# Copying the sources' columns of one tile in every 12th group on VectorE and on ScalarE, in a graph layer's edge loop

## The chip, the core and the metric

The kernel runs on one core of a Trainium2 chip. The metric is the device time of one execution in microseconds (us). In the profiles PE is TensorE's matmul array and PEld its weight loads, DVE is VectorE, ACT is ScalarE, POOL is GpSimd and SP is SyncE. L372 is line 372 of the kernel.

## The reference

A graph network's layer over 12500 nodes with 64 features and 212500 edges with 32 features, in float32. The edges come sorted by their destination `dst`.

```python
msg_in = concatenate([x[src], x[dst], edge_attr_32], axis=-1)        # 212500 x 160
messages = relu(msg_in @ mW1 + mb1) @ mW2 + mb2
aggregated = segment_sum(messages, dst, num_segments=12500)
u = relu(concatenate([x, aggregated], axis=-1) @ uW1 + ub1) @ uW2 + ub2
out = layernorm(x + u, axis=-1, eps=1e-05)
```

`src` is random over the nodes, so the rows `x[src]` have to be gathered, edge by edge.

## The kernel before

**Tiling.** Edges are cut into tiles of 128 (P) and tiles into groups of three (TG), so that there are 554 groups (G). All sorted destinations of a group lie in a window of 32 (W) nodes. A group's work has these steps:

- *gather* (L142 to L153): POOL issues one indirect DMA for each tile, L145, which brings the 128 source rows of 64 numbers to `own.s`, one edge on each partition. `own.s` is a ring of 20 groups (RING). The gather of group g waits for the copy of group g - 20 out of the ring (`copy_by[g - RING]`). The loop issues it 16 groups ahead (AHEAD).
- *onehot* (L321, work at L324): DVE writes, beside each gathered row, 32 numbers that say which node of the window the edge goes to.
- *turn* (L354): PE transposes the three tiles of `own.s`, 96 columns each (64 features and 32 of the one-hot), into PSUM, L360; ACT copies the result to `own.st` and takes the row sums of the one-hot part, L372.
- *hidden* (L381): PE multiplies the turned group with the weights, L392, and ACT applies relu, L401.
- *sums* (L411): PE multiplies hidden values with the one-hots, L419 and L422; DVE adds the result to `agg` and the window's counts to a row of `xc`, L431 and L432.
- *windows* and *places* (L306 and L291), once for four groups: PE computes the destinations' part for four windows, L310, DVE copies it into the weights `own.wm`, L315; DVE reads the places of the next four windows and copies their nodes' columns, L303.

**Copied tiles.** The features of all nodes also lie transposed in SBUF, in `xc`, one column a node. In some groups, the keys of COPIED, the third tile (ONE) isn't gathered. Its 128 columns are copied one at a time from `xc` to a tile `own_f`, by DVE with `tensor_copy` (L349) or by ACT with `activation` (L350). The source's number comes from a register: a load (L343) fills eight registers (REGS) from `cols_sb`. Each way has a range of groups, BY_DVE and BY_ACT, whose step is also the number of groups over which the 128 columns are spread, and two tiles `own_f`. The copying ends three groups (SLACK) before the group itself:

```python
at = k - (g - SLACK - way.step)
if not 0 <= at < way.step:
    continue
f, used, ahead = source_columns(g), g - 2 * way.step, held[engine]
for r in range(at * P // way.step, (at + 1) * P // way.step):
    if r % REGS == 0:
        ...
    column = f[:D, r : r + 1], xc[:D, bass.ds(ahead[r % REGS], 1)]
```

For a copied group the gather loop leaves out that tile (L150). ACT's copy of the turned group becomes two instructions, one for the 64 feature rows of two tiles and one for the 32 one-hot rows of three (L369). In *hidden* PE makes two products for the copied tile, one of `own_f` with the weights and one of the 64 remaining rows of `own.st` (L389).

**Order.** The order of each engine's work is written out by hand. In iteration k of the main loop come, in this order: the load of edge features (SP), *places* when k leaves 1 over 4, *onehot* of group k + 1, a PE step, the gathers of group k + 16, and the columns that are due in k (`copies_of`, L334). The PE step (`step`, L502) holds *turn* of group k, *hidden* of k - 2 and *sums* of k - 4 in one stretch with one wait ahead and one semaphore at its end; *windows* is added to it for every fourth k. When it is done, ACT does the copy of turn and the relu of hidden, and DVE the addition of sums, and the copies to `own.wm` if there are any. So DVE's queue reads: addition of step k, columns of k, *places* if due, one-hot of k + 2, addition of step k + 1. PE's step k + 2 waits for that one-hot. ACT's queue reads: copy, relu, columns. Every 22 groups or so, when all edges of 512 nodes are done, an *update* (L438) computes the output of those nodes, in steps between the others.

Of the kernel before, what the change touches and what calls it, by code (L numbers as in the profile page):

```python
# [31 lines left out]
G = (E + GE - 1) // GE  # L32
# [11 lines left out]
NEAR_GROUPS = 24  # L44
SHORT = 10
ONE = TG - 1
BY_DVE = range(44, G - 16, 16)
BY_ACT = range(48, G - 16, 24)
COPIED = {**dict.fromkeys(BY_DVE, (ET.DVE, BY_DVE)), **dict.fromkeys(BY_ACT, (ET.Activation, BY_ACT))}
SLACK = 3  # L50
REGS = 8
# [30 lines left out]
class Own:  # L82
# [4 lines left out]
    def __init__(self, nc, ctx):  # L87
        def on(name, *shape, of=nc.sbuf_tensor):
            return ctx.enter_context(of(name, list(shape), F32)).ap()
# [6 lines left out]
        self.f = {way: [on(f"own_f{len(way)}_{i}", P, P) for i in range(2)]  # L96
                  for way in (BY_DVE, BY_ACT)}
        self.ident = on("own_ident", P, P)
# [797 lines left out]
```

## Time and profile before

| | |
|---|---|
| median of 3 runs | 2696.31 us (2695.68 to 2698.4) |
| the profiled execution | 2690.72 us, span 2688.9 us |
| mean granted clock of TensorE | 0.787 |
| gathers L145 | 1609, mean 944 ns |
| copied columns | 3968 on DVE (mean 143 ns), 2688 on ACT (mean 193 ns) |
| register loads L343 | 496 on DVE (median 608 ns), 336 on ACT (median 551 ns) |
| turned tiles L360 | 1661 |

A row of the groups reads: line, engine, operation, what it writes and reads, how often, then busy us and mean ns of one, then the idle time of the engine just ahead of it and who ended most of it. A row of the timeline reads: start and duration in us, engine, line, operation, how many were merged into the row, and in brackets the idle time ahead of it and its end. The ends of matmuls are modelled. DVE and ACT overlap their short instructions, so that eight columns take less than eight times the mean of one.

The page's slices show how even the run is:

```profile
PE   1356666666666675766666656666566666677667
PEclk9777787778777777777777878787777777787779
```

The first line is PE's busy share in 40 equal slices in tenths, the second the granted clock, in tenths of full speed. From the third slice to the last two, nothing changes.

### The profile page before, as it was taken

How to read it: one execution, taken by the hardware profiler on the slowest of the kernel's cores; microseconds unless marked ns; L12 is line 12 of the kernel's file. 1: busy time of each engine (PE TensorE's matmuls, PEld its weight loads, DVE VectorE, ACT ScalarE, POOL GpSimd, SP SyncE). 2: the span in 40 equal slices, each digit the busy share in tenths (PEclk: the TensorE clock that was granted, in tenths of full speed). 3: DMA queues.
4: the chain of work that ended last, by engine and by line, in shares of the span. 5: the costliest groups of instructions: out<-in, count | busy, mean ns of one | idle time of the engine just before them, and what ended most of it. 6: DMA issues, size and time to landing. Idle time of an engine off the chain costs nothing.

```text
span 2688.9 us, 45023 instructions
## 1 busy us (share of the span) xinstructions
PE 1687.1 (63%) x9545; PEld 1457.1 (54%) x9545; DVE 1060.2 (39%) x7163; ACT 827.3 (31%) x4455; POOL 1519.4 (57%) x1616
## 2 busy tenths in 40 slices
PE   1356666666666675766666656666566666677667
PEld 0355555555555565655555555555555555565555
DVE  4124344344443444443434434434344343443423
ACT  0123333333333333333333333333333333333322
POOL 7565555555555555555555555555555555565550
PEclk9777787778777777777777878787777777787779
DMA  3211111111111111111111111111111111111110
GB/s 80 58 44 32 35 32 36 31 36 32 35 37 32 34 34 35 31 36 32 37 31 35 34 32 34 34 34 34 35 32 34 33 37 31 35 35 35 33 34 14
DMA packets 71878, 95.29 MB, mean 35 GB/s; under 512 B 32633, under 2 KB 40076, under 8 KB 71596
## 3 DMA queue, kind: packets, MB, share of 16 engines
q0 software_dynamic: 51488, 52.80, 10.3%
q1 hardware_dynamic: 19193, 39.06, 5.3%
q8 instruction: 81, 1.33, 0.2%
q14 instruction: 202, 1.65, 0.2%
q10 hardware_dynamic: 914, 0.46, 0.1%
HBM read 88.90 MB, written 3.20 MB: 34 GB/s over the span
## 4 chain that ended last, share of the span: by engine, by line
PE 50%; issue 18%; another core or an unknown queue 16%; ACT 10%; ACTq 3%; DVE 3%; DMA 0%; DVEq 0%; SPq 0%
PE own_ps L422 19%; PE own_ps L392 16%; PE own_ps L360 9%; ACT own_h L401 3%; ACT own_f L350 3%; ACT own_st L372 3%; ACTq L343 2%; PE own_ps L419 2%; PE u_ps L462 2%; PE u_ps L449 1%; PE own_ps L310 1%; ACTq L350 1%; PE u_ps L450 1%; DVE agg L431 1%
## 5 line engine op out<-in xcount | busy, mean ns | idle before, releaser
L145 POOL DMA_INDIRECT own_s<-in_x,src_sb x1609 | 1518.6, 944 | 1091.0 <-ACT own_st L372 677.1
L360 PE MATMUL own_ps<-own_ident,own_s 128*96 128x128 f32 x1661 | 364.2, 341 | 906.5 <-issue 677.0
L372 ACT ACTIVATE own_st<-own_ps 96x384 f32<-96x384 f32 (+2 forms) x606 | 286.1, 472 | 1697.7 <-PE own_ps L422 1006.0
L360 PEld LDWEIGHTS own_ps<-own_ident,own_s 128*96 128x96 f32 x1661 | 224.4, 159 | 983.9 <-issue 735.6
L422 PE MATMUL own_ps<-own_s,own_h 128*128 128x128 f32 x3322 | 647.5, 343 | 0.4 <-issue 0.3
L392 PE MATMUL own_ps<-own_wm,own_st 128*128 128x128 f32 (+1 forms) x3322 | 630.8, 338 | 1.4 <-DVE own_wm L315 1.4
L392 PEld LDWEIGHTS own_ps<-own_wm,own_st 128*128 128x128 f32 (+1 forms) x3322 | 571.9, 251 | 16.5 <-issue 11.7
L431 DVE TENSOR_TENSOR agg<-own_ps,agg 128x32 f32 x554 | 105.2, 190 | 1202.7 <-ACT own_h L401 1089.6
L422 PEld LDWEIGHTS own_ps<-own_s,own_h 128*128 128x128 f32 x3322 | 525.6, 236 | 27.3 <-issue 0.3
L349 DVE COPY own_f<-xc 64x1 f32 x3968 | 428.8, 143 | 217.7 <-issue 213.2
L350 ACT ACTIVATE own_f<-xc 64x1 f32 x2688 | 304.6, 193 | 9.1 <-issue 6.2
L401 ACT ACTIVATE own_h<-own_ps 128x384 f32<-128x384 f32 x553 | 263.3, 476 | 18.4 <-PE own_ps L392 13.1
L315 DVE COPY own_wm<-own_ps 32x128 f32<-32x128 f32 x550 | 156.9, 285 | 6.8 <-issue 1.3
L324 DVE TENSOR_TENSOR own_s<-iota,dlc 128x96 f32<-128x96 f32 x554 | 135.7, 245 | 21.6 <-issue 16.7
L432 DVE TENSOR_TENSOR xc<-own_ps,xc 1x32 f32 x554 | 101.2, 183 | 27.8 <-PE u_ps L450 7.4
L419 PE MATMUL own_ps<-own_ident,own_counts 32*1 32x32 f32 x554 | 107.1, 193 | 4.2 <-ACT own_st L372 1.9
L372 ACT ACTIVATION_READ_ACCUMULATOR own_st<-own_ps 96x1 f32 (+1 forms) x554 | 106.4, 192 | 0.6
L303 DVE COPY xw<-xc 66x32 f32 x554 | 78.6, 210 | 49.2 <-issue 48.3
L419 PEld LDWEIGHTS own_ps<-own_ident,own_counts 32*1 32x1 f32 x554 | 41.3, 74 | 93.8 <-issue 47.8
L310 PE MATMUL own_ps<-w1b,xw 66*128 66x128 f32 (+1 forms) x276 | 56.9, 290 | 0.0
L462 PE MATMUL u_ps<-u,u 128*128 128x64 f32 (+1 forms) x196 | 49.1, 398 | 10.0 <-ACT u L452 10.0
L462 PEld LDWEIGHTS u_ps<-u,u 128*128 128x128 f32 (+1 forms) x196 | 47.5, 326 | 11.5 <-ACT u L452 11.3
(63 smaller groups left out, 338.5 us busy)
## 6 DMA issues: line engine op xcount, KB each, us to landing
own_st<-in_efT SPq DMA_DIRECT2D x138, 192.0 KB
own_s<-in_x,src_sb POOLq DMA_INDIRECT x1609
xin<-in_x SPq DMA_DIRECT2D x24, 128.0 KB
out<-o SPq DMA_DIRECT2D x24, 128.0 KB
xc<-in_xT SPq DMA_DIRECT2D x12, 179.2 KB
dlc_i<-in_dst_cols SPq DMA_DIRECT2D x1, 831.0 KB
xc<-in_xT SPq DMA_DIRECT2D x4, 179.5 KB
src_sb<-in_src SPq DMA_DIRECT2D x13, 50.5 KB
```

The lines of the kernel that those rows point to most:

```text
L145: nc.gpsimd.indirect_dma_start(out=s[:p, j, :D], out_offset=None, in_=x[:, :], in_offset=bass.IndirectOffsetOnAxis(ap=src_sb[:p, g * TG + ...
L315: c = nc.vector.tensor_copy(wm[g % NW][D : D + W, :], wp[i * W : (i + 1) * W, :])
L324: places_by[g] = nc.vector.tensor_tensor(own.s[g % RING][:, :, D:], iota.unsqueeze(1).to_broadcast([P, TG, W]), dlc[:, g * TG : (g + 1) * ...
L349: c = (nc.vector.tensor_copy(*column) if engine == ET.DVE else nc.scalar.activation(*column, AF.Copy))
L350: else nc.scalar.activation(*column, AF.Copy))
L360: nc.tensor.transpose(xt[:, j * P : j * P + p], s[:p, j, :], ident[:p, :p])
L372: nc.scalar.activation(t[to, c : c + m], xt[to, :m], AF.Copy, **({"accum_out": counts[to, g : g + 1]} if to.stop > D else {})), step)
L392: did.append(nc.tensor.matmul(pre[:p, j, :], edges, weights, start=i == 0, stop=i == len(parts) - 1))
L401: relu_by[g] = [nc.scalar.activation(h, pre, AF.Relu)]
L419: did = [nc.tensor.transpose(line, counts[lo:, g : g + 1], ident[lo : D + W, lo : D + W])]
L422: did.append(nc.tensor.matmul(sg, h[:p, j, :], s[:p, j, D:].unsqueeze(1).to_broadcast([p, TIMES, W]), start=j == 0, stop=j == len(sizes) - 1))
L462: nc.tensor.matmul(o_ps[:p, k], u[:, k:q:n], u2, start=True, stop=True)
```

## The change

```diff
-BY_DVE = range(44, G - 16, 16)
-BY_ACT = range(48, G - 16, 24)
+BY_DVE = range(44, G - 16, 12)
+BY_ACT = range(50, G - 16, 12)
```

G - 16 is 538. Before, DVE copies the third tile of groups 44, 60, ... 524, 31 tiles, and ACT that of 48, 72, ... 528, 21 tiles. After, DVE copies that of 44, 56, ... 536, 42 tiles, and ACT that of 50, 62, ... 530, 41 tiles. The 128 columns of a tile are spread over 12 groups in place of 16 on DVE and 24 on ACT: 10 or 11 columns a group in place of 8 on DVE and 5 or 6 on ACT. The buffers, the ring, the lead of the gathers and the size of a register load stay. `cols_sb` has a row for each copied tile and grows with their number.

## The prediction

> **What bounds it now.** I read the page's busy line, then its groups, then the table of waits, then the timeline of one stretch, row by row.
>
> ```profile
> PE 1687.1 (63%) x9545; PEld 1457.1 (54%) x9545; DVE 1060.2 (39%) x7163; ACT 827.3 (31%) x4455; POOL 1519.4 (57%) x1616
> L145 POOL DMA_INDIRECT own_s<-in_x,src_sb x1609 | 1518.6, 944 | 1091.0 <-ACT own_st L372 677.1
> L349 DVE COPY own_f<-xc 64x1 f32 x3968 | 428.8, 143 | 217.7 <-issue 213.2
> L350 ACT ACTIVATE own_f<-xc 64x1 f32 x2688 | 304.6, 193 | 9.1 <-issue 6.2
> ```
>
> No engine is full. The table of waits shows a ring of waits: POOL waits for ACT's copy of a turned group, ACT for a PE step, DVE for ACT's relu.
>
> ```profile
> DVE agg L431 <- ACT own_h L401: 1089.6, 280, 47.6
> ACT own_st L372 <- PE own_ps L422: 1006.0, 245, 8.2
> POOL own_s L145 <- ACT own_st L372: 677.1, 274, 8.7
> ```
>
> PE's own waits for one-hots carry "issue" in this table, so I matched the starts of its steps with the ends of L324 rows: of 490 steps (30 to 519), 288 start 0.07 us after a one-hot ends, 178 follow the step before without a gap. So DVE's chain (add, columns, one-hot) is one half of the ring. The other half shows only in the timeline, here from the release of the pair 200, 201 to that of 204:
>
> ```profile
> 1031.16 0.49 ACT L372 ACTIVATE own_st<-own_ps 96x384 f32<-96x384 f32 x1 [5.29 <-PE own_ps L422]
> 1032.15 0.19 DVE L431 TENSOR_TENSOR agg<-own_ps,agg 128x32 f32 x1 [4.61 <-ACT own_h L401]
> 1032.48 1.18 DVE L315 COPY own_wm<-own_ps 32x128 f32<-32x128 f32 x4
> 1033.69 0.57 DVE L349 COPY own_f<-xc 64x1 f32 x8
> 1035.14 0.26 DVE L324 TENSOR_TENSOR own_s<-iota,dlc 128x96 f32<-128x96 f32 x1
> 1035.49 0.85 PE L360 MATMUL own_ps<-own_ident,own_s 128*96 128x128 f32 x3 [5.70 <-issue]
> 1039.37 0.49 ACT L372 ACTIVATE own_st<-own_ps 96x384 f32<-96x384 f32 x1 [5.41 <-PE own_ps L422]
> 1040.22 0.94 POOL L145 DMA_INDIRECT own_s<-in_x,src_sb  x1 [1.68 <-ACT own_st L372]
> ...
> 1041.34 0.95 DVE L349 COPY own_f<-xc 64x1 f32 x8 [0.57 <-issue]
> 1044.55 0.39 PE L310 MATMUL own_ps<-w1b,xw 66*128 66x128 f32 x2
> 1046.45 0.94 POOL L145 DMA_INDIRECT own_s<-in_x,src_sb  x1 [0.30 <-issue]
> 1048.99 0.87 ACT L372 ACTIVATE own_st<-own_ps 64x256 f32<-64x256 f32 x2 [5.48 <-remote]
> 1050.34 0.94 POOL L145 DMA_INDIRECT own_s<-in_x,src_sb  x1 [2.94 <-ACT own_st L372]
> ```
>
> PE's last matmul of step 204 ends at 1044.94, yet ACT takes it at 1048.99: 4.05 us late, and 1.60 us after POOL's run of six gathers ended (1047.39). This is the rule: of 182 steps whose matmuls end over 3.5 us into a run, the median was taken 1.55 us after the run's end (middle half 1.48 to 1.64); steps that end in the first 3 us of a run pass at once (0.04 us). Why, the trace doesn't say. So POOL is in the ring: release, ACT's copy, 0.87 us later a run of 6 gathers 1.25 us apart, 1.55 us, next release. The kernel goes in pairs of groups.
>
> Taking times from one L372 copy to that of the group two later (groups 40 to 484, nearly all paired like this), I get two kinds of halves. **Even** (starts at a group divisible by 4, the one with the weight copies L315): 6 gathers and no copied group 9.48 us (32 halves, 8 in 10 between 9.45 and 9.54: POOL's run); 5 gathers 8.52 (25; here DVE's chain and PE's step end it); a copied group turned at its start 9.8 to 10.0 (46; ACT's copy is split, 0.50 us later for POOL, and PE has two passes more). **Odd** (starts two later): 6 gathers 9.57 with or without copied work near it. Means 9.43 and 9.55, 56.9 us for 12 groups.
>
> **The change, part by part.** By its ranges, 42 + 41 = 83 tiles are copied, 31 more than 31 + 21.
>
> Gathers: 31 fewer, 1578. What one is worth depends on its run. Before, all copied groups are divisible by 4 (44 + 16i, 48 + 24i), so each shortened an even half, from 9.48 to 8.52. Now DVE's (44 + 12i) stay there, and ACT's (50 + 12i) leave 2 over 4: their gather leaves the odd run, where 4 us of slack stand behind POOL. One gather less is 1.25 there: 9.55 to 8.30. The least it could be worth is nothing, if DVE's chain ends that half.
>
> Splitting ACT's copy: 31 more. Rows 1039.37 to 1040.22 and 1048.99 to 1050.34 give POOL's start 0.85 and 1.35 after the copy's, so 0.50. ACT's copied groups now pay it at the start of an odd half: 9.55 to 10.05. Their two extra PE passes fall on a step with 4 us of slack: nothing; without that cover about 0.7 (two rows of 128x128 and the pause, at the slow rate of 0.21 a pass).
>
> DVE's columns: 1408 more, 10.67 for 8 in a group. Uncovered, eight take 0.95 (0.115 each beyond the first); behind L315, whose 1.18 us let DVE's sequencer run ahead, 0.57 (0.061 each). A register load for eight takes 0.61 (median of its 496 rows); before, it stood ahead of each batch of eight, now it falls inside the batch, and in 4 of 12 batches there are two. An uncovered batch costs 0.31 + 0.2 to 0.6 more. In odd halves the 4 us cover this; with that gone it is 0.5 to 0.9 a group. In even halves of 6 gathers, 9.48 against about 8.4 for the chain leaves 1.1: covered too. Two in three even halves are ended by the chain. At groups 0 over 12 (5 gathers) the batch is columns 74 to 84, one load, started under L315: +0.3 (from 0.16, columns alone, to 0.6). At 8 over 12 (copied group turned, 6 gathers, 10.0 now) it is columns 32 to 41, the second load after the eighth column and with the load for the windows queued behind it: 0.61 + two columns, +0.8 (0.2 to 1.2). The later one-hot, hence PE's step, hence ACT's copy, hence POOL's run are all late by that.
>
> ACT's columns: 2560 more, 10.67 for 5.33, at 0.093 spacing 0.5 us a group and 0.55 a load. From a copy's start ACT would be busy some 2.1 us instead of 1.5. The next copy comes 2.6 to 3.4 us later within a pair that is not held, so it fits; where both of a pair are released at once, the second waits 0.6 more, but POOL needs it only 3.75 us into its run. I take nothing; uncovered it would be 0.5 a pair, 130 us at the very worst.
>
> The Trainium skill speaks against more DVE copies: "SBUF — State Buffer", section "Who interferes with whom", says that a copy in a two-port mode locks GpSimd out of the port through which it writes descriptors. The row here: in 396 places where a column copy alone overlaps the start of a gather, the pause before it is the usual 0.305. By the rule the 1408 columns would delay POOL by up to 1408 x 0.14 = 200 us (an estimate); by the row by nothing, and I go by the row.
>
> Sum for 12 groups. Even: 8.52 + 0.3; 9.48; 10.0 + 0.8. Odd: 10.05; 8.30; 9.55. Together 57.0, against 56.9: +0.1, times 41 periods +4 us. The 25 updates add: odd halves with one are 0.65 longer already (10.09 against 9.44), and with 0.5 us more on DVE a group and a shorter run in one of three I take 0.3 more each, +7 us. So +11 on the profiled 2690.7 (2688.9 span), which was 5.6 below the median of 2696.3: **2707 us**.
>
> **The rivals.** *The pairs shift (faster).* From group 485 on the kernel pairs 1 with 2 and 3 with 0 (over 4); there a group takes 4.59 us against 4.74 before it. In that pairing the copied group is the second of its pair, so its split copy delays no run, and both kinds of removed gathers count in full (there halves with 6 gathers take 9.45 to 9.55 and with 5 8.05): 57.0 - 1.4 - 1.25 = 54.3 for 12 groups, 2.6 us less. The flip needs one lone run, which comes when the second of a pair is late; a later chain makes that likelier. It decides from about five periods on (it must make up 11 us); over 15 of 41 it gives 2707 - 40 = 2667, over all 2600. Against it: in the trace it stayed only once. *The columns are paid wherever DVE ends PE's wait (slower).* If the slack that I counted is used up, as by updates or by a second of a pair that misses the first 3 us of a run and is held to its end, each of the 288 steps pays 0.5: 144 us, 2850; half of that, 2780. For it: 288 of 490; against: odd halves lie within 0.1 us although their one-hots vary by over 0.5. *The gathers win alone (faster).* If the batches cost only their columns under L315 (0.16 for both kinds), 57.0 falls by 0.8 a period: 2674.
>
> **How the numbers follow.** Near balance, as computed (2691 to 2740): 0.45. Faster by a shift or by the gathers: 0.37. The chain as the bound (2740 and up): 0.18. A measurement of this kernel tells about 0.2% (5.4 us) from no change. The forecast's own case spreads over 2690 to 2725, of which a fourth lies within 5.4 us of 2696: faster 0.38, same 0.12, slower 0.50. The bounds of the unknown costs (0.44 and 0.9 below and above for the two batches, 1.25 for the odd gather) times 41 are about -55 and +65; I keep **2650 to 2765**.
>
> **What would show it.** Right: odd halves at 6, 2 and 10 over 12 of about 8.3, 10.05 and 9.55; even ones at 8 over 12 near 10.8; POOL idle after a run still ended by ACT's copy; 1578 gathers. Wrong: odd halves of 5 gathers near 9 (DVE's chain ended them), more runs of three gathers, or long stretches paired 1 with 2. A changed gather pause beside columns would make the port rule right after all.

## The result, and the profile after

The kernel after takes 2761.29 us (2757.41 to 2763.33, four runs) against 2695.99 of the kernel before beside it: a ratio of 1.0241, 95% interval 1.0224 to 1.0259. It is 2.4% slower, 65 us, where +11 was forecast. The profiled execution took 2760.6 us (span 2758.9); TensorE's granted clock is 0.758 after 0.787.

The busy line and the three groups of copies and gathers after (busy time, mean ns of one | idle time before them, what ended most of it):

```profile
PE 1791.9 (65%) x9607; PEld 1542.0 (56%) x9607; DVE 1219.3 (44%) x8571; ACT 1117.8 (41%) x7046; POOL 1494.5 (54%) x1585
L145 POOL DMA_INDIRECT own_s<-in_x,src_sb x1578 | 1493.7, 947 | 1185.7 <-ACT own_st L372 771.1
L349 DVE COPY own_f<-xc 64x1 f32 x5376 | 586.8, 144 | 516.9 <-issue 503.3
L350 ACT ACTIVATE own_f<-xc 64x1 f32 x5248 | 567.7, 193 | 74.8 <-issue 67.1
```

POOL saved 25 us of work and waits 94 us longer for ACT's copy of a turned group (677.1 before). The idle time ahead of DVE's column copies has risen from 213 to 503 us, while ACT's 2560 further columns brought 66 us of idle time ahead of ACT's. "issue" means that no semaphore is waited for: in those gaps stand register loads and register instructions, which the page doesn't count as busy. The table of waits after (us in total, times, longest):

```profile
POOL own_s L145 <- ACT own_st L372: 771.1, 300, 8.1
...
DVE agg L431 <- ACT own_h L401: 701.5, 302, 50.0
DVE own_f L349 <- issue: 503.3, 834, 2.0
...
DVE xw L303 <- issue: 95.1, 180, 2.6
```

DVE's wait for ACT's relu, its reserve, has shrunk by 388 us, from 1090 to 702. Where that has gone, the timeline after shows (the batch of columns 32 to 41, with *places* behind it):

```profile
1048.34 1.18 DVE L315 COPY own_wm<-own_ps 32x128 f32<-32x128 f32 x4
1049.55 0.57 DVE L349 COPY own_f<-xc 64x1 f32 x8
1050.71 0.26 DVE L349 COPY own_f<-xc 64x1 f32 x2 [0.59 <-issue]
1051.92 0.18 DVE L303 COPY xw<-xc 66x32 f32 x1 [0.95 <-issue]
1052.66 0.18 DVE L303 COPY xw<-xc 66x32 f32 x1 [0.56 <-issue]
1053.38 0.29 DVE L303 COPY xw<-xc 66x32 f32 x2 [0.54 <-issue]
1053.88 0.26 DVE L324 TENSOR_TENSOR own_s<-iota,dlc 128x96 f32<-128x96 f32 x1 [0.21 <-issue]
...
1054.24 0.85 PE L360 MATMUL own_ps<-own_ident,own_s 128*96 128x128 f32 x3 [4.72 <-ACT own_st L372]
```

The eight columns and the gap of 0.59 for the second register load are as forecast. New is what follows: the four L303 copies, which need a register instruction each and take 0.56 us in one go where nothing disturbs them, stretch over 1.75 us (1051.92 to 1053.67). Ahead of the first and the third stand the load for the windows (0.72 us) and register instructions recorded with some 0.7 us in place of the usual 0.05. The one-hot waits behind all that, and PE's step behind the one-hot: the row of PE names ACT's copy as its releaser, but the step's first weights load at 1054.21, 0.07 us after the one-hot's end.

In the list of one line's instructions the duration is min/median/max in ns. The register instructions of the column copies and of the window copies after:

```profile
L349 DVEq FUSED_REGOPS  x5376: 3/46/987, 219.1 to 2677.7; - x200
```
```profile
L303 DVEq FUSED_REGOPS  x554: 4/46/726, 37.4 to 2729.2; - x185
```

The usual one is 46 ns. I counted those over 200 ns, on all lines of DVE, and call them slow: 341 of them, 225.5 us (before: 44, 25.8 us). Of these, 293 fall to runs of six gathers: they begin 4.5 us or more after the run's start (it is 7.2 long), and end at most 1.47 us after it. That is the part of a run in which PE's completions are held back too. The recorded time isn't a price, though. Of the 280 slow ones on L349, taken in order with the copies that they serve, 271 have their copy begun before the recorded end and 178 even before the recorded start; the copy of column 41 starts at 1050.83, its register instruction by the record at 1051.17. What the trace shows for certain is that copies come late there, such as the three of L303 with 0.7 us between their starts. Nor are there more held steps than before: ACT takes 176 of PE's 490 steps (30 to 519) over 1 us after their last matmul, against 280.

### The profile page after: what moved, and what is told of

It reads as the page before. It is cut to its first block, busy times and chain, and to the rows that moved or that the text cites. A ratio compares the mean times of both kernels' runs of the same rounds, so it can differ in the third digit from the quotient of the medians.

```text
span 2758.9 us, 53542 instructions
## 1 busy us (share of the span) xinstructions
PE 1791.9 (65%) x9607; PEld 1542.0 (56%) x9607; DVE 1219.3 (44%) x8571; ACT 1117.8 (41%) x7046; POOL 1494.5 (54%) x1585
## 4 chain that ended last, share of the span: by engine, by line
PE 47%; issue 24%; ACT 11%; another core or an unknown queue 7%; ACTq 4%; DVE 2%; DVEq 0%
PE own_ps L422 17%; PE own_ps L392 16%; PE own_ps L360 9%; ACT own_f L350 5%; ACT own_st L372 3%; ACTq L343 3%; ACT own_h L401 2%; PE own_ps L419 2%; PE u_ps L462 1%; PE own_ps L310 1%; ACTq L350 1%; PE u_ps L449 1%; PE u_ps L450 1%; DVE stats L468 1%
## 5 line engine op out<-in xcount | busy, mean ns | idle before, releaser
L145 POOL DMA_INDIRECT own_s<-in_x,src_sb x1578 | 1493.7, 947 | 1185.7 <-ACT own_st L372 771.1
L360 PE MATMUL own_ps<-own_ident,own_s 128*96 128x128 f32 x1661 | 381.4, 354 | 894.5 <-issue 724.7
L372 ACT ACTIVATE own_st<-own_ps 96x384 f32<-96x384 f32 (+2 forms) x637 | 298.7, 469 | 1422.2 <-PE own_ps L422 754.1
L349 DVE COPY own_f<-xc 64x1 f32 x5376 | 586.8, 144 | 516.9 <-issue 503.3
L422 PE MATMUL own_ps<-own_s,own_h 128*128 128x128 f32 x3322 | 682.4, 357 | 1.0 <-issue 1.0
L392 PE MATMUL own_ps<-own_wm,own_st 128*128 128x128 f32 (+1 forms) x3322 | 674.0, 353 | 1.4 <-DVE own_wm L315 1.4
L392 PEld LDWEIGHTS own_ps<-own_wm,own_st 128*128 128x128 f32 (+1 forms) x3322 | 607.6, 264 | 22.1 <-issue 14.6
L350 ACT ACTIVATE own_f<-xc 64x1 f32 x5248 | 567.7, 193 | 74.8 <-issue 67.1
L422 PEld LDWEIGHTS own_ps<-own_s,own_h 128*128 128x128 f32 x3322 | 555.8, 248 | 28.9 <-issue 0.6
L303 DVE COPY xw<-xc 66x32 f32 x554 | 78.2, 191 | 96.2 <-issue 95.1
L372 ACT ACTIVATION_READ_ACCUMULATOR own_st<-own_ps 96x1 f32 x554 | 106.4, 192 | 1.0
```

The costliest lines, as they stand in the source:

```text
L145: nc.gpsimd.indirect_dma_start(out=s[:p, j, :D], out_offset=None, in_=x[:, :], in_offset=bass.IndirectOffsetOnAxis(ap=src_sb[:p, g * TG + ...
L349: c = (nc.vector.tensor_copy(*column) if engine == ET.DVE else nc.scalar.activation(*column, AF.Copy))
L350: else nc.scalar.activation(*column, AF.Copy))
L360: nc.tensor.transpose(xt[:, j * P : j * P + p], s[:p, j, :], ident[:p, :p])
L372: nc.scalar.activation(t[to, c : c + m], xt[to, :m], AF.Copy, **({"accum_out": counts[to, g : g + 1]} if to.stop > D else {})), step)
L392: did.append(nc.tensor.matmul(pre[:p, j, :], edges, weights, start=i == 0, stop=i == len(parts) - 1))
```

## The experiments

The runs fell on several chips, and each is compared with the kernel before on its own. Two of these chips behave as in the prediction (before 2693 and 2657 to 2661 us). On two others the kernel before takes 2038 to 2039 us: there ACT takes a step a median 0.04 us after its last matmul, and no register instruction is slow, in each of the traces from there. Ratios from the first two are told beside each other; the other two are a different machine for this question.

**On a chip without held completions: the two halves of the change.** ScalarE's range one group later, the gathers of ScalarE's tiles put back, and each engine's part alone:

```diff
 e1:  BY_ACT = range(51, G - 16, 12)
 e2:  ... if not copied(g, j) or g in BY_ACT      (L150)
 e3:  BY_ACT = range(48, G - 16, 24)
 e4:  BY_DVE = range(44, G - 16, 16)
```

> ACT's copied groups are 51 + 12i in place of 50 + 12i, so they leave 3 over 4 and the gather left out is in the second group of an odd run: 3 + 2 in place of 2 + 3. Theory A (a run that begins with two gathers ends before the next group's copy is there, and the pair breaks): pairs hold again, lone runs fall from 92 to under 40, 2690 to 2705 us. Theory B (DVE's longer queue reaches into the late part of POOL's run, where its register instructions take 0.7 us in place of 0.05): nothing of that changes, 2740 to 2765 us, over 250 slow register instructions on DVE.

> The changed kernel, but the third tile of ACT's 41 copied groups is gathered as well (its rows are overwritten by nothing and used by nothing): all odd runs have six gathers, all column copies stay. Theory A: more gathers, yet faster, 2695 to 2720 us. Theory B: no gain, 2755 to 2780 us.

> Only DVE's part of the change: 42 tiles by DVE in every 12th group, ACT's 21 in every 24th as before. Theory A: no run begins with two gathers in an odd half, 2685 to 2705 us. Theory B: most of the loss is here, 2735 to 2760 us, and over 200 slow register instructions on DVE (44 before, 341 after the change).

> Only ACT's part of the change: 41 tiles by ACT in groups 50 + 12i, DVE's 31 in every 16th as before. Theory A: most of the loss is here, 2735 to 2760 us, over 70 lone runs. Theory B: 2685 to 2705 us, under 80 slow register instructions on DVE.

Measured, against 2038.11: e1 1.0722 [1.0669, 1.0775], e2 1.1178 [1.1114, 1.1241], VectorE's part alone 1.0953 [1.0919, 1.0988], ScalarE's part alone 0.9878 [0.9862, 0.9894]. The times expected were made for a chip as in the prediction and can't be held against these, and e1 and e2 lack the kernel after beside them. But the signs of e3 and e4 separate the parts: VectorE's is the loss, ScalarE's a gain. The profile of ScalarE's part alone there:

```profile
L145 POOL DMA_INDIRECT own_s<-in_x,src_sb x1589 | 1501.6, 945 | 485.2 <-issue 358.9
```
```profile
POOL own_s L145 <- issue: 358.9, 1178, 0.3
```

POOL waits for nothing but its own 0.30 us between gathers: 1589 gathers in a single run. There the 20 gathers fewer bring 25.5 us, 1.28 each, their full spacing. With VectorE's part alone POOL's busy share is 68% in place of 75, and the single run is broken into 83 (a run ends at a pause of over 1 us): 362 of PE's 490 steps (30 to 519) start right after a one-hot, against 263 with ScalarE's part alone. No slow register instruction is in it, as the list of one line's instructions for VectorE's part alone shows:

```profile
L349 DVEq FUSED_REGOPS  x5376: 46/46/53, 122.0 to 2151.8; - x200
```

So VectorE's batches can lose time without slow register instructions.

**The kernels again on a chip with held completions, a new order, and longer loads.** f1 and f2 are the kernels before and after. f3 is the kernel after with another order on DVE's queue; f4 loads 16 registers at once.

```diff
 f3, in the main loop:
+    onehot(1)                             ahead of the loop
-        if k % SB == 1:
-            places(k // SB + 1)
-        onehot(k + 1)
         ... the step ...
+        if (k + 1) % SB == 1:
+            places((k + 1) // SB + 1)
+        onehot(k + 2)
         if k + AHEAD < G:
             gather(k + AHEAD)
         copies_of(k)
 f4:
-REGS = 8
+REGS = 16
```

> The kernel before, for its trace beside the next ones. In the last four runs it took 2038 us and their DVE had no slow register instruction at all. Where that is so, theory C (two limits: POOL's gathers back to back, 1609 x 1.249 = 2010 us, or DVE's chain between a PE step and the next one-hot): one run of over 1500 gathers, 2030 to 2045 us. Where PE's steps are held behind POOL's runs as in the profile before: 2690 to 2700 us, some 280 runs.

> The changed kernel, for its trace and time beside the others. Theory C: DVE's chain is the limit, 0.5 us a group longer, 2160 to 2290 us against 2038 (6 to 12% slower), POOL waits. Theory H (the loss comes from the held steps and the slow register instructions only): within 1% of the kernel before wherever these are absent.

> The changed kernel with DVE's order changed: the places and the one-hot of group k + 2 stand ahead of the columns of k, so that PE's step k + 2 doesn't wait for the columns; the work is the same. Theory C: the loss is gone and the fewer gathers count, 1985 to 2035 us where the kernel before takes 2038, under 2690 where it takes 2696. Theory H: no better than the changed kernel.

> The changed kernel with register loads for sixteen columns in place of eight: 336 loads on DVE in place of 672. If the loads that now fall inside a batch are the larger part of what C counts: half of the loss against the kernel before is gone. If the columns are: over 80% of the loss stays.

Measured, against 2656.56: f2 2726.59, 1.0254 [1.0231, 1.0277], the result repeated on another chip, with 246 slow register instructions against 21. The kernel before lies in neither of the spans expected for f1, and those for f2 were for a chip without held completions. **f3 2611.5, 0.9823 [0.9803, 0.9842]: faster than both kernels.** f4 1.0348 [1.0319, 1.0377]. The timeline of f3 at such a batch:

```profile
1037.09 0.19 DVE L431 TENSOR_TENSOR agg<-own_ps,agg 128x32 f32 x1 [3.76 <-ACT own_h L401]
1037.42 1.18 DVE L315 COPY own_wm<-own_ps 32x128 f32<-32x128 f32 x4
1038.63 0.56 DVE L303 COPY xw<-xc 66x32 f32 x4
1039.22 0.26 DVE L324 TENSOR_TENSOR own_s<-iota,dlc 128x96 f32<-128x96 f32 x1
1039.40 1.21 DVE L349 COPY own_f<-xc 64x1 f32 x10
1039.58 0.84 PE L360 MATMUL own_ps<-own_ident,own_s 128*96 128x128 f32 x3 [5.61 <-ACT own_h L401]
```

The windows' copies and the one-hot follow the addition at once (1037.09 to 1039.48), and the columns come behind, where they make only the next addition late if at all. The page's groups of f3 beside that:

```profile
L145 POOL DMA_INDIRECT own_s<-in_x,src_sb x1578 | 1494.2, 947 | 1037.5 <-ACT own_st L372 614.9
L349 DVE COPY own_f<-xc 64x1 f32 x5376 | 589.1, 143 | 457.7 <-issue 449.1
```

POOL's wait for ACT's copy is down to 615 us (746 in f2). But DVE still idles 449 us ahead of the columns (450 in f2), and 343 register instructions are slow (215.6 us), more than in f2. So their number isn't the loss; it is what is queued behind them. Theory C was right here, and theory H, by which the order gains nothing, wrong.

f4's loads are half as many and nearly twice as long (the first row is of the kernel after, the second of f4):

```profile
L343 DVEq TENSOR_LOAD <-cols_sb x672: 4/604/840, 218.4 to 2676.2; - x168
L343 DVEq TENSOR_LOAD <-cols_sb x336: 4/1106/1414, 216.2 to 2674.6; - x168
```

Half by half (from one L372 copy to that of the group two later, groups 40 to 480, means): the half that starts at group 8 over 12 (a group whose number leaves 8 when divided by 12), whose batch had two loads and now has one, takes 10.89 us instead of 11.41; the one at 0 over 12, whose load of 16 falls behind the sixth of its 11 columns as the load of 8 did, takes 10.09 instead of 9.36, and the one at 6 over 12, with a load inside as well, 8.30 instead of 7.45. A load costs time where it stands between a batch's columns, and more the longer it is. The loss didn't halve with the number of loads, it grew by 0.9%.

**The parts, on a chip with held completions.** The two parts, ScalarE's later start, and f3's order with the tiles of the kernel before:

```diff
 g1:  BY_ACT = range(48, G - 16, 24)
 g2:  BY_DVE = range(44, G - 16, 16)
 g3:  BY_ACT = range(51, G - 16, 12)
 g4:  f3 with both ranges of the kernel before
```

> DVE's part of the change alone: DVE's range from 44 every 12th group as after, ACT's range as before (48, every 24th): 63 tiles copied, 1598 gathers. Theory A (on a chip whose completions are held, the added column batches on DVE are the loss; ACT's part is nearly neutral): ratio 1.015 to 1.035 to the kernel before, over 200 register instructions of DVE of 0.2 us and more (12 to 44 before), lone runs few (under 60). Rival B (the loss is the odd half's missing gather, which ends a run before the pair's second copy and breaks the pair; DVE's batches are covered): ratio 0.995 to 1.008.

> ACT's part of the change alone: ACT's range from 50 every 12th group as after, DVE's range as before (44, every 16th): 72 tiles copied, 1589 gathers. Theory A: ratio 0.990 to 1.006 (on the chip without held completions it was 0.988). Rival B (odd gathers break the pairs): ratio 1.012 to 1.03, with 70 to 100 runs of one to three gathers as in the kernel after.

> The kernel after with ACT's range from 51 in place of 50: the copied tile's group is the one behind the pair's first, so the gather that is saved and the split copy fall on other places of the pair, with the same counts. Theory A: DVE's batches are the same, so the ratio stays within 0.008 of the kernel after's on such a chip (1.024 and 1.025): 1.017 to 1.033. Rival B: the runs break elsewhere, the ratio moves by over 0.01, most likely down, to 1.00 to 1.015.

> The order of the kernel that was faster than both (windows' register loads and the one-hot of two groups on issued behind the step and ahead of the column copies) with the tiles of the kernel before (52). Theory C (the order is the gain: one-hots no longer end PE's wait, whatever the tiles; the 31 further tiles are then worth their gathers, 31 x 1.25 = 39 us at most, 0 to 1.5% of it seen): ratio 0.985 to 0.997, PE's steps begun right after a one-hot under 60 of 490. Rival D (the order and the tiles each give about half): 0.990. Rival E (the order alone gains nothing, as POOL's runs of six then end each half; only with fewer gathers does it show): 0.998 to 1.003.

Measured, against 2693.49: VectorE's part alone 1.0303 [1.0277, 1.0329], ScalarE's part alone 0.9935 [0.9913, 0.9957], ScalarE from 51 1.0126 [1.0105, 1.0147], the order with the old tiles 0.9837 [0.9817, 0.9856]. The two parts multiply to 1.0236, the whole change's 1.0241. Theory A is right on both ratios; the runs of one to three gathers, 25 before and 93 after, which rival B put down to ScalarE's part, are 35 in it and 39 in VectorE's: only the two together make them many. On g3 rival B is right: one group later is worth 1.2% beside VectorE's batches, with 61 such runs. By halves (sum of six 57.75 us in place of the kernel after's 58.56, on another chip) 0.58 of it comes from the half at 2 over 12, 9.75 in place of 10.33. The copied group is then the second of its pair, and by the prediction's rival of the shifted pairs its split copy delays no run; that fits, but nothing else tests it. For VectorE's part alone the table of waits and the groups say the same as for the kernel after:

```profile
DVE own_f L349 <- issue: 397.7, 699, 1.3
```
```profile
L145 POOL DMA_INDIRECT own_s<-in_x,src_sb x1598 | 1509.7, 945 | 1175.3 <-ACT own_st L372 753.9
```

It has 155 slow register instructions, fewer than the 200 expected and half as many as the kernel after, and yet the whole of the loss. ScalarE's part alone has 194, where under 80 had once been expected, and is faster than the kernel before. g4 shows that the order, not the number of tiles, is f3's gain: 0.984 with 52 tiles, 0.982 with 83 (on another chip; the expectations write 82). Its expected count was wrong, though: 218 steps of PE still start right after a one-hot, and 302 in f3, against 288 before. The one-hot still is the last thing that a step waits for; it only comes earlier.

**What in a batch costs.** h1 takes the loads and register instructions from VectorE's batches by reading fixed columns; h2 puts the 672 loads back, with one register instruction each. h3 and h4 are f3's order with ScalarE's part alone and with ScalarE from 51:

```diff
 h1:
-                if r % REGS == 0:
+                if r % REGS == 0 and engine != ET.DVE:
-                column = f[:D, r : r + 1], xc[:D, bass.ds(ahead[r % REGS], 1)]
+                column = f[:D, r : r + 1], (xc[:D, r : r + 1] if engine == ET.DVE
+                                            else xc[:D, bass.ds(ahead[r % REGS], 1)])
 h2:  loads as after; fixed columns if engine == ET.DVE and r % REGS
 h3:  f3 with BY_DVE = range(44, G - 16, 16)
 h4:  f3 with BY_ACT = range(51, G - 16, 12)
```

> The kernel after with VectorE's 5376 column copies reading fixed columns 0 to 127 of the table, so that VectorE has neither their 672 register loads nor their 5376 register instructions (it computes other sources for the tiles of VectorE's groups; everything else as after, 1578 gathers). Theory L (the register load inside the batch, 0.6 us, is most of what the batch costs): ratio 0.975 to 0.99 here and h2 with the loads back at 1.01 to 1.025. Theory Q (the register instructions are most of it, slow ones above all): ratio 0.975 to 0.99 here and h2 within 0.006 of it. Theory V (the copies themselves, 8 to 11 times 0.06 us, are most of it): 1.01 to 1.02 in both.

> As h1, but the first column of every eight is read at its loaded address: the 672 register loads are back and 672 of the 5376 register instructions (other sources for the other seven; everything else as after). Theory L: 1.01 to 1.025, near the kernel after. Theory Q: within 0.006 of h1. Theory V: 1.01 to 1.02 in both.

> The order that was faster than both (windows' loads and the one-hot of two groups on ahead of the column copies) with ACT's part of the change alone (VectorE's range as before; 72 tiles, 1589 gathers). If what was measured apart adds up (order with the old tiles 0.984, ACT's part 0.9935): 0.975 to 0.98. If the order hides all that the columns cost, so that only the number of gathers counts, it lies within 0.004 of the order with all 82 tiles (0.982): 0.98 to 0.986.

> The same order with all 82 tiles, ACT's range from 51 in place of 50. Before the order was changed, 51 in place of 50 gave 1.2% (1.0126 against 1.024). If that gain was of the pairs (fewer lone runs): 0.968 to 0.977 here. If it was of DVE's chain, which the order has already relieved: 0.979 to 0.986.

Measured, against 2660.74: h1 0.9848 [0.9832, 0.9865], h2 1.0005 [0.9988, 1.0022], h3 0.9850 [0.9834, 0.9867], **h4 0.9778 [0.9762, 0.9795], the fastest kernel**. With f2 of the same chip (1.0254) the batch comes apart: adding the loads takes 1.6% (42 us; 0.06 for each of 672), and the 4704 further register instructions beside them 2.5% (66 us). No theory of a single item holds: loads and register instructions both count, and without them the loss is gone, with all 5376 copies in place. What the copies themselves cost isn't measured, since the kernel before has loads and register instructions of its own. The column copies in the groups of h1, then of h2, then of f2:

```profile
L349 DVE COPY own_f<-xc 64x1 f32<-64x1 f32 x5376 | 373.6, 136 | 31.9 <-issue 10.8
```
```profile
L349 DVE COPY own_f<-xc 64x1 f32<-64x1 f32 (+1 forms) x5376 | 410.2, 137 | 257.2 <-issue 244.4
```
```profile
L349 DVE COPY own_f<-xc 64x1 f32 x5376 | 586.1, 143 | 462.8 <-issue 449.9
```

The idle time goes from 11 us to 244 with the loads and to 450 with the register instructions. The lower granted clock of TensorE, 0.758 after 0.787 in the two profiles, doesn't bring the loss by itself: on this chip h1 has 0.768 to 0.774, the kernel before beside it 0.777 to 0.788, and h1 is the faster one.

ScalarE's part alone in the new order (h3, 0.985) is no better than all 83 tiles (0.982), as the second of its expectations had it, which fits that the order hides what the columns cost. h4 gains 0.3% on f3 by the times (2603.5 and 2611.5 us), 0.45% by the ratios, and lies just outside either expected span; the pairs and the chain aren't separated by it.

**The worth of the gathers.** The tiles of the kernel before with light batches, as in h1, run twice:

```diff
 i1, i2:  h1 with both ranges of the kernel before
```

> The kernel before (52 tiles, 1609 gathers) with VectorE's 3968 column copies reading fixed columns, so without their 496 register loads and 3968 register instructions (other sources for the tiles of VectorE's groups). With the same taken from the kernel after (1578 gathers) the ratio was 0.985. If the 31 gathers fewer are worth what they free of POOL's runs once the batches are light (g: ACT's part alone gave 0.65%), this run lies 0.5 to 1.5% above that one: 0.990 to 1.0. If the whole gain of that run came from the light batches and the gathers are worth nothing: 0.981 to 0.988.

> The same kernel as the run before (52 tiles, no register loads and register instructions in VectorE's column batches, other sources for the tiles of VectorE's groups), which fell on the chip where the kernel before takes 2038 us and POOL's 1609 gathers are the bound; there it changed nothing (1.000). On a chip whose completions are held: 0.990 to 1.0 if the 31 gathers fewer are worth something once the batches are light, 0.981 to 0.988 if they are worth nothing.

Both fell on a chip where POOL's 1609 gathers bound the kernel (1.0000 and 0.9998), and decide nothing for the others. What 31 gathers are worth on a chip with held completions, once the batches are light, stays open. Nor was it tried what makes completions late and register instructions slow.

## Why the prediction was right or wrong

The sign and the range held; the size did not. +11 was forecast, +65 came; the rival "the columns are paid wherever DVE ends PE's wait" was nearer, with +84 at half its size. That the range held is in part luck: the time lies 4 us under its upper end, and the range doesn't follow from the terms. By their own bounds the two batches span 0.74 us a period below and 0.70 above, and the odd gather 1.25 above, which gives -30 and +80 us, not -55 and +65. Measured on the halves of a pair (us, means over groups 40 to 480, updates in them; the forecast's even halves are without one, its odd ones start from the mean of 9.55 with them; the last two columns are g1 and g2):

| half starts at, over 12 | before | forecast | after | VectorE alone | ScalarE alone |
|---|---|---|---|---|---|
| 0 | 9.78 | 8.82 | 9.48 | 10.01 | 9.68 |
| 2 | 9.57 | 10.05 | 10.33 | 9.61 | 10.17 |
| 4 | 9.15 | 9.48 | 9.78 | 9.36 | 9.51 |
| 6 | 9.69 | 8.30 | 7.56 | 9.47 | 7.83 |
| 8 | 9.38 | 10.8 | 11.82 | 10.75 | 9.87 |
| 10 | 9.38 | 9.55 | 9.57 | 9.58 | 9.52 |
| sum | 56.95 | 57.0 | 58.56 | 58.8 | 56.6 |

The sum is 1.6 us a period above before, and 1.6 times 41 is the loss. Above the forecast stand 0.66 at 0 over 12 (27 us in 41 periods), 0.30 at 4, 0.28 at 2, and 0.28 at 6 and 8 together: the first term is the largest, but not the whole miss.

- **The failed term: "At groups 0 over 12 (5 gathers) ... +0.3 (from 0.16, columns alone, to 0.6)".** This half came at 9.48, 0.66 over the forecast and outside its upper bound. VectorE's part alone has it too: its halves of five gathers without a copied turn (at 0 and 4 over 12) take 9.22 us against 8.58, +0.64. The sum knew the copies' spacing and the load. On the chip of h1 and h2 such halves take 8.41 us in the kernel before; this one takes 8.42 with the copies alone (h1), 8.86 with the loads (h2) and 9.36 with the register instructions as well (f2). So copies and loads together are +0.45, inside the term's bounds, and the step that failed is the price of the register instructions: 0.5 us more, where the sum had them only as a part of the 0.061 us a column that a quiet place shows.
- **"Covered too", for even halves of six gathers.** 9.78 against 9.48: 0.30 a period that was counted at nothing. With VectorE's part alone it is 9.64 against 9.49. The cover of 1.1 us was the difference of two typical times; what used it up isn't shown.
- **"8 over 12, +0.8".** Confirmed where it stands alone: halves that turn a copied group with six gathers go from 9.99 to 10.75 us in VectorE's part alone, +0.76. In the kernel after the half takes 11.82, and the one before it takes less.
- **"One gather less is 1.25 there: 9.55 to 8.30".** It came at 7.56 (7.83 in ScalarE's part alone), but not as a gain of its own. Runs of one to three gathers rise from 25 to 93, one of the prediction's own signs of being wrong; the likely reason, not tested by itself, is that the run behind the copied group has two gathers, ends before the next group's copy is there, and so breaks the pair. What the half saves, the next one pays: 7.56 and 11.82 are 19.4 together, 19.1 was forecast.
- **The split copy, +0.50.** 10.33 after, 10.17 in ScalarE's part alone, 10.05 forecast: right to 0.12 where VectorE's batches are the old ones.
- **"ACT's columns: 2560 more ... I take nothing".** Nothing speaks against it: all 2560 of them are in ScalarE's part alone, and it is 0.65% faster, with 20 gathers fewer.
- **The pairs that shift.** This rival didn't come: of 181 runs of five and more gathers in the trace after that begin in groups 40 to 484, 145 stand behind the copy of a group that leaves 0 or 2 over 4, and only 4 behind one that leaves 1.
- **The port rule.** The Trainium skill's page "SBUF — State Buffer", section "Who interferes with whom", which the prediction weighed, has DVE's copies in a two-port mode lock GpSimd out. In the trace after, 471 gathers have column copies and no other work of DVE beside them. They take 0.946 us on average, the 630 beside no column copy 0.948, and the pause where a gather inside a run begins beside a column copy alone (254 times; 343 before by this count, where the prediction has 396) is again 0.305 us: the row was the one to go by. In which mode these copies ran, no run here shows.

The mechanism was thus near: the ring of waits is as forecast, and so are two of the three even halves, at 0 and 8 over 12 and not at 4, as places where VectorE's batches cost time. What was mis-sized is DVE's queue. There the prediction costed what an instruction needs in a quiet place and took the rest as hidden, though 288 of 490 steps were waiting for that very queue.

## What to carry to other kernels

In a queue that ends another engine's wait, it counts less how much work is added than whether it stands ahead of what is waited for: the kernel with these batches ahead of the one-hot is 2.4% slower than before, and with the one-hot ahead of them 1.8% faster, 2.2% with ScalarE's tiles one group later. Most of that gain is the order's own, 1.6% with the old tiles. Cost a small copy with its register instruction and its share of the register load, neither of which counts as busy: taking these two away and leaving the copies took the kernel from 1.025 to 0.985. And try the two halves of a change apart: one of these was a gain.

## What was not expected of the hardware

- A register instruction of DVE is recorded with 46 ns, and some with about 0.7 us: in the kernel after, and in runs of six gathers, only from 4.5 us into the run to 1.5 us behind it. In h1 and h2, with at most 672 of them on L349, there is none that is slow, not even among those of L303, whose code is the same (18 of 554 in the kernel after):

```profile
L303 DVEq FUSED_REGOPS  x554: 46/46/53, 34.7 to 2585.5; - x185
```

  So it takes more than a run of gathers; what, these runs don't say.
- The kernel before takes 2038, 2657 or 2693 us, by the chip, at granted clocks of TensorE of 0.88 to 0.92, 0.78 to 0.80 and 0.78 to 0.79. On chips of the first kind the traces have no slow register instruction and completions are as a rule taken at once, POOL's gathers are the bound of the kernel before, and VectorE's part costs 9.5% in place of 3.0%, ScalarE's gains 1.2% in place of 0.65%. A change of this size has to be weighed on more than one chip.
- A register load of DVE takes 0.604 us for eight and 1.106 us for 16 registers. The Trainium skill's page "DMA: Bandwidth & Descriptors", section "Latency and other measured facts", gives a floor of some 600 ns; the first agrees, and from eight to 16 registers it is 0.063 us a register more.
